# First image by half chunks, low rows loaded ahead into any stored place, and a reordered seam in a scan-then-pointwise kernel

## The chip, the cores and the metric

The kernel runs on one core of one Trainium2 chip. The metric is device time in microseconds (us). The core has a matmul engine (TensorE, PE in the profile, PEld for its weight loads), a vector engine (VectorE, DVE), an activation engine (ScalarE, ACT), a general engine (GpSimd, POOL) and a queue that only issues transfers (SyncE, SP). Each executes its own instruction list in order, and they meet at semaphores. Transfers between DRAM and on-chip memory are issued from SP, ACT or POOL and run on 16 shared DMA engines.

## What is computed

The input is 16 images of 128 channels by 64 x 64, float32. There are two residual layers, each on a group-normalised copy of its input (groups of 4 channels over a whole image):

```python
# layer 0: x = x + diagonal_lstm(_gn(x))    a scan over skewed columns, 64 rows in parallel
# layer 1: x = x + quantum_conv(_gn(x))     pointwise: each pixel on its own
xq = xf @ pre_w.T + pre_b                   # 128 channels -> 4 angles
z = _simulate(xq, q_weights)                # 4 qubits, 2 layers, expectation of Z
out = z @ post_w.T + post_b                 # 4 -> 128 channels
```

Layer 1's normalisation needs the mean and variance of each whole image after layer 0, so no pixel of layer 1 can start before layer 0's last pixel is known.

## The kernel before

**Storage.** Forty of the 64 rows of every image live on chip in `ring`, a tile of 10 blocks of 4 rows. The first 24 rows ("low rows") are finished early by the scan, are written out to a DRAM scratch `low`, and their blocks take the last 24 rows. In layer 1 an image is 8 chunks of 512 pixels (256 KB): chunks 0 to 2 (`k < NT`, with `NT` = 3) are low rows that must be loaded again, chunks 3 to 7 are pairs of blocks in `ring`.

**Layer 0** is 160 scan steps (`step`), bound by TensorE. After the last step, `residual(NSTEP - 1, ...)` adds the last diagonal to `x` in place (L618, on POOL), `late_sums` on POOL (L685 to L689) has gathered moments of the last rows, and the *seam* closes the statistics. A strip of the last 4 columns is summed on DVE (L894 to L898), TensorE adds the group sums (L883), DVE and ACT make `rstd2` (L902 to L904, then L149 to L153), DVE scales the angle weights of image 0 (`image_weights`, L913), and TensorE makes `mr_ps` (L925) for the bias `b_image` (L926). `fill()` (L183) is a matmul of 512 columns whose output nobody reads: one stands ahead of the strip's sum and two behind it.

**Layer 1**, per image `b`, all in an order written out by hand (`tc.manual_schedule()`: every engine gets its instructions in program order):

- `angles(b)`, PE L962: 8 matmuls of 32 output rows by 512 columns make the 128 angle rows `theta` from the 8 chunks. A float32 matmul shows as two records.
- `sines(b)`: ACT adds the bias (L976), DVE reduces to a turn (`near` L978, subtraction L979), ACT takes the sine (L982).
- `squares(b)`: 2 matmuls to amplitudes (`am`, L990) and 2 squares on ACT (L1002).
- `outputs(b, h)`, h = 0, 1: 4 matmuls `po` (L1008) into 4 PSUM banks, one per chunk.
- `finish(b, h, po)`: for each chunk, DVE adds output, bias and `x` in place (L1025), and SP stores it to `out_dram` (L1027).

The loop body for image `b` is `outputs(b,0)`, first half of `sines(b+2)`, `finish(b,0)`, loads, `squares(b+1)`, `outputs(b,1)`, `finish(b,1)`, `angles(b+3)`. The angles of an image are therefore made while three images are in flight.

**Low rows in layer 1.** The 48 low chunks go through 14 fixed places: 8 `spare` tiles and 6 `lowp` tiles. Chunks 0 to 13 are loaded in the seam, some from SP during the last steps, six from POOL. Later chunks always take the place of the chunk 14 before:

```python
lows[n] = spare[n % NBUF] if n % NBUF < 8 else lowp.tile(...)      # NBUF = 14
for n in range(NBUF + NT * b, min(NBUF + NT * b + NT, NT * NB)):   # in the loop, after finish(b, 0)
    load(n)                                                        # a DMA issued from POOL
```

Each such load waits on POOL until the store of the chunk that held the place has landed. The places of `ring` chunks are stored once and not used again.

Of the kernel before, what the change touches and what calls it, by code (L numbers as in the profile page):

```python
# [11 lines left out]
F32 = mybir.dt.float32  # L12
AF = mybir.ActivationFunctionType
# [3 lines left out]
P = 128  # L17
NB = 16
# [7 lines left out]
BLOCK = ROWS * NW  # L26
CHUNK = 2 * BLOCK
# [7 lines left out]
NSTEP = BAND + NW + SLOTS - 1  # L35
# [45 lines left out]
def kernel(  # L81
# [29 lines left out]
    NT = NLOW * NW // CHUNK  # L111
    low = dram.tile([NB, P, NLOW * NW], F32, name="low")
# [43 lines left out]
    with ExitStack() as scan:  # L156
# [5 lines left out]
        bias = wpool.tile([P, 4], F32, name="bias")  # L162
# [4 lines left out]
        xns, hst = ([v.rearrange("p (q n) -> p q n", q=2) for v in spare[i : i + 2]] for i in (4, 6))  # L167
# [8 lines left out]
            ps = pool.tile([P, v.shape[-1]], F32, name=nc.get_next_instruction_name(), tag=tag)  # L176
            nc.tensor.matmul(ps, lhsT=wsT[:, 0:P], rhs=v, start=True, stop=True)

        def fill():

            ps = ps_gate.tile([P, 512], F32, name=nc.get_next_instruction_name(), tag="gate")
            v = w_amp.rearrange("p h n -> p (h n)").unsqueeze(1).to_broadcast([P, 2, 256])
            nc.tensor.matmul(  # L183
                ps.rearrange("p (k n) -> p k n", k=2), lhsT=w_out, rhs=v, start=True, stop=True
            )

        def inv_step(j, pool):

# [27 lines left out]
        with ExitStack() as prep:  # L216
# [139 lines left out]
            for i in range(2):  # L356
                v = ws_n[i]
# [43 lines left out]
            first = {}  # L401
# [150 lines left out]
        def by_pairs(v, q, j, n):  # L552
            v = v[:, q, j * NB : (j + n) * NB]
            return v if n == 1 else v.rearrange("p (k h i) -> p k h i", h=2, i=NB)
# [53 lines left out]
            if a1 < b:  # L608
                nc.gpsimd.tensor_sub(diff[:, 0, a1:b], now[:, 1, a1 - NB : b - NB], now[:, 0, a1:b])  # L609

        def residual(t, new):

            for band in range(2):
                s0, s1 = slots(t, band)
                for q in range(2):
                    j0, j1 = (s0 + 1 - q) // 2, (s1 + 1 - q) // 2
                    for j, n, x1 in diagonal(t, band, q, j0, j1):
                        nc.gpsimd.tensor_add(x1, x1, by_pairs(new, q, j, n))  # L618
# [238 lines left out]

        def low_rows(queue, n, v):
            b, k = n // NT, n % NT
            queue.dma_start(out=v, in_=low[b, :, k * CHUNK : (k + 1) * CHUNK])  # L860

        waiting = []
        begin(nc.gpsimd.tensor_copy, cst, 0, cinv, 0)
# [1 line left out]
        with tc.manual_schedule():  # L865
# [6 lines left out]
            for later in sums:  # L872
                for _ in later:
                    pass
            residual(NSTEP - 1, hst[NSTEP % 2])
            low_rows(nc.sync, 6, spare[6])

            warm = small.tile([P, 1], F32, name="warm", tag="inv_t")
# [3 lines left out]
            def add(to, w, v, start=False):  # L882
                nc.tensor.matmul(to, lhsT=w, rhs=v, start=start, stop=True, skip_group_check=True)  # L883

            add(ps, by_half, moments, True)
            for h in range(2):
                add(ps, by_half, added[:, :, :, h])
                add(ps[:, 1], by_one, inner[:, :, h])
            fill()

            v = ring[:, block(NH - ROWS)].rearrange("p i (r w) -> p i r w", w=NW)[:, :, :, NW - STRIP :]
            d, sq = (work.tile([P, NB, ROWS, STRIP], F32, name=f"strip{i}", tag=f"both{i}") for i in range(2))
# [9 lines left out]
            nc.vector.tensor_copy(m, ps[:, 0])  # L902
            nc.vector.scalar_tensor_tensor(var, m, -1.0, m, ALU.mult, ALU.mult)
            nc.vector.scalar_tensor_tensor(var, var, EPS, ps[:, 1], ALU.add, ALU.add)  # L904
            for _ in range(2):
                fill()
            inverse_root(small, var, rstd2, 2)

            nc.scalar.activation(warm, shift, AF.Sin)
# [20 lines left out]

    lowp = ctx.enter_context(tc.tile_pool(name="lowp", bufs=6))
    sinp = ctx.enter_context(tc.tile_pool(name="sinp", bufs=3))
    nearp = ctx.enter_context(tc.tile_pool(name="nearp", bufs=1))
    sqp = ctx.enter_context(tc.tile_pool(name="sqp", bufs=2))
# [2 lines left out]
    ps_o = ctx.enter_context(tc.tile_pool(name="ps_o", bufs=1, space=PSUM))  # L939
    ths, turns, sqs = {}, {}, {}  # L940

    NBUF = 14
    lows = {}

    def load(n):

        lows[n] = spare[n % NBUF] if n % NBUF < 8 else lowp.tile([P, CHUNK], F32, name=f"low{n}", tag="low")
        if n >= 8:
            low_rows(nc.gpsimd, n, lows[n])

    def rows_of(b, k):
        if k < NT:
            return lows[NT * b + k]
        q = block(2 * ROWS * k)
        return ring[:, q : q + 2, b, :]

    def angles(b):
        th = ps_t.tile([P, CHUNK], F32, name=f"theta{b}", tag="theta")
        for h in range(2):

            for j in (2, 3, 1, 0):
                nc.tensor.matmul(  # L962
                    th[32 * j : 32 * j + 32, :],
                    lhsT=w_image[:, b, 16 - 16 * h : 48 - 16 * h],
                    rhs=rows_of(b, 2 * j + h),
                    start=(h == 0),
                    stop=(h == 1),
                    tile_position=(0, 32 * j),
                )
        ths[b] = th  # L970

    def sines(b):

        th = ths[b]
        y = sinp.tile([P, CHUNK], F32, name=f"y{b}", tag="y")
        nc.scalar.activation(y, th, AF.Identity, bias=b_image[:, b : b + 1])  # L976
        near = nearp.tile([P, CHUNK], F32, name=f"near{b}", tag="near")
        nc.vector.tensor_scalar(near, y, ROUND, ROUND, ALU.add, ALU.subtract)  # L978
        nc.vector.tensor_sub(y, y, near)  # L979
        turns[b] = y  # L980
        yield
        nc.scalar.activation(y, y, AF.Sin, scale=TWO_PI)  # L982

    def squares(b):
        ams = []
        for h in range(2):
            am = ps_a.tile([P, CHUNK], F32, name=f"am{b}_{h}", tag=f"am{h}")

            k = 64 * h
            nc.tensor.matmul(  # L990
                am,
                lhsT=w_amp[k : k + 64, h, :],
                rhs=turns[b][k : k + 64, :],
                start=True,
                stop=True,
                tile_position=(k, 0),
            )
            ams.append(am)

        sqs[b] = [sqp.tile([P, CHUNK], F32, name=f"sq{b}", tag="sq"), turns[b]]  # L1000
        for am, s in zip(ams, sqs[b]):
            nc.scalar.activation(s, am, AF.Square)  # L1002

    def outputs(b, h):
        po = [ps_o.tile([P, CHUNK], F32, name=f"po{b}_{h}_{j}", tag=f"po{j}") for j in range(4)]
        for j in range(4):
            k = 32 * j
            nc.tensor.matmul(  # L1008
                po[j],
                lhsT=w_out[k : k + 32, :],  # L1010
                rhs=sqs[b][h][k : k + 32, :],
                start=True,
                stop=True,
                tile_position=(k, 0),
            )
        return po

    def finish(b, h, po):
        for j in range(4):
            k = 4 * h + j  # L1020
            x1 = rows_of(b, k)
            y = po[j]
            if k >= NT:
                y = y.rearrange("p (k n) -> p k n", n=BLOCK)
            nc.vector.scalar_tensor_tensor(x1, y, b_out, x1, ALU.add, ALU.add)  # L1025
            o = ov[b, :, k * CHUNK : (k + 1) * CHUNK]
            nc.sync.dma_start(out=o if k < NT else o.rearrange("c (k n) -> c k n", n=BLOCK), in_=x1)  # L1027

    def idle():

# [73 lines left out]
```

## Time and profile before

| what | value |
|---|---|
| runs (3): median, lowest, highest | 1425.06, 1423.18, 1426.97 us |
| profiled execution: time, span of its instructions | 1422.99, 1421.1 us |
| mean granted TensorE clock | 0.997 |
| busy share of the span: PE, DVE, POOL, ACT | 96%, 69%, 65%, 55% |
| layer 1, first store issued to end of span | 1299.21 to 1421.1 us |
| in that stretch: mean rate of all transfers | 349 GB/s |

The runs differ among themselves by 0.27%; the profiled execution is 2.07 us under the median of the runs, and its span leaves out 1.89 us of its time. All positions below are us from the start of the span. "Share" of DMA is the mean busy share of the 16 DMA engines.

### The profile page before, as it was taken

Reading aid. Unit: us, or ns where it says so; the run is one execution under the profiler, and the core shown is the slowest. Engines: PE = TensorE matmul, PEld = TensorE weight load, DVE = VectorE, ACT = ScalarE, POOL = GpSimd, SP = SyncE. Lnnn points to the kernel's source line nnn. Section 1 sums busy time; section 2 is a strip of 40 time slices with the busy share of each in tenths; the row PEclk is TensorE's granted clock in tenths of the full one; section 3 lists DMA queues with packets and bytes.
Section 4 is the critical chain, followed back from the end, with each engine's and each line's share of the span. In section 5 each row is a group of like instructions: output and inputs, shape, how many; then the busy total and the mean of one; then the engine's idle time right before and its main releaser. Section 6 shows DMA issues by size and latency. Waiting matters only on the chain. (4 is left out here: it accounts for less than half of the span.)

```text
span 1421.1 us, 20142 instructions
## 1 busy us (share of the span) xinstructions
PE 1364.6 (96%) x5970; PEld 964.5 (68%) x5970; DVE 981.4 (69%) x2538; ACT 778.0 (55%) x1856; POOL 921.9 (65%) x1824
## 2 busy tenths in 40 slices
PE   6778999999999999999999999999999999888998
PEld 5658887777767777667666777776667778783332
DVE  7983555566665666887777776666665567866877
ACT  4555666555555555555555555555555566543331
POOL 4226887777667777788877776777777777762120
PEclk9999999999999999999999999999999999999999
DMA  9970000000000000133333100000000000005999
GB/s 332 368 272 1 1 2 0 1 1 1 1 0 1 0 1 1 59 119 119 119 119 119 60 1 1 0 1 1 1 1 0 2 1 1 31 9 200 369 373 324
DMA packets 88013, 107.05 MB, mean 75 GB/s; under 512 B 5424, under 2 KB 72016, under 8 KB 87904
## 3 DMA queue, kind: packets, MB, share of 16 engines
q1 hardware_dynamic: 83264, 94.39, 19.4%
q0 software_dynamic: 3408, 10.58, 2.2%
q8 instruction: 48, 0.79, 0.2%
q10 hardware_dynamic: 1232, 0.80, 0.2%
q14 instruction: 61, 0.50, 0.1%
HBM read 59.61 MB, written 46.14 MB: 74 GB/s over the span
## 5 line engine op out<-in xcount | busy, mean ns | idle before, releaser
L584 PE MATMUL ps<-spare,wxT 128*128 128x512 f32 (+18 forms) x1280 | 479.6, 518 | 0.7 <-POOL spare L575 0.7
L768 DVE TENSOR_TENSOR ps<-ps,both 128x256 f32<-128x256 f32 (+9 forms) x544 | 221.8, 409 | 304.7 <-PE ps L753 303.1
L772 ACT ACTIVATE ps<-ps,bias 128x512 f32<-128x512 f32 (+23 forms) x480 | 279.3, 583 | 220.2 <-DVE ps L768 183.7
L753 PE MATMUL ps<-spare,w1T 128*128 128x256 f32 (+16 forms) x1272 | 345.8, 353 | 9.9 <-DVE spare L835 4.9
L584 PEld LDWEIGHTS ps<-spare,wxT 128*128 128x128 f32 x1280 | 230.9, 190 | 173.2 <-issue 155.5
L753 PE MATMUL ps<-spare,w0T 128*128 128x256 f32 (+16 forms) x1272 | 343.8, 352 | 0.8 <-POOL spare L609 0.8
L803 ACT COPY both<-ps 128x256 f32<-128x256 f32 (+9 forms) x544 | 191.6, 355 | 180.7 <-PE ps L753 161.1
L618 POOL TENSOR_TENSOR ring<-ring,spare 128x256 f32<-128x256 f32 (+8 forms) x488 | 248.1, 540 | 31.2 <-DVE stats L706 21.0
L753 PEld LDWEIGHTS ps<-spare,w1T 128*128 128x128 f32 x1272 | 229.8, 190 | 35.7 <-DVE spare L835 7.6
L753 PEld LDWEIGHTS ps<-spare,wsT 128*128 128x128 f32 x1088 | 194.8, 190 | 86.4 <-DVE spare L835 34.7
L753 PE MATMUL ps<-spare,wsT 128*128 128x256 f32 (+14 forms) x1088 | 241.3, 365 | 5.4 <-DVE spare L835 3.7
L753 PEld LDWEIGHTS ps<-spare,w0T 128*128 128x128 f32 x1272 | 230.3, 190 | 22.1 <-POOL spare L609 0.9
L575 POOL TENSOR_TENSOR spare<-spare,rstd 128x512 f32<-128x512 f32 (+10 forms) x160 | 171.0, 1069 | 14.8 <-DVE rstd L153 2.3
L570 POOL TENSOR_TENSOR spare<-ring 128x256 f32<-128x256 f32 (+8 forms) x213 | 147.5, 703 | 0.0
L829 ACT ACTIVATE g<-cst 128x256 f32<-128x256 f32 (+20 forms) x320 | 103.1, 369 | 64.4 <-DVE cst L828 63.8
L835 DVE TENSOR_TENSOR spare<-g,ps 128x256 f32<-128x256 f32 (+17 forms) x319 | 105.6, 369 | 43.8 <-ACT g L829 41.9
L565 POOL TENSOR_TENSOR spare<-ring,mean 128x16 f32<-128x16 f32 (+8 forms) x247 | 131.3, 541 | 5.8 <-DVE mean L143 5.6
L609 POOL TENSOR_TENSOR spare<-spare 128x240 f32<-128x240 f32 (+9 forms) x136 | 102.7, 755 | 29.5 <-DVE spare L835 25.7
L772 ACT ACTIVATE g<-ps,bias 128x512 f32<-128x512 f32 (+20 forms) x160 | 97.4, 609 | 27.1 <-DVE ps L768 21.1
L828 DVE TENSOR_TENSOR cst<-cst,ps 128x256 f32<-128x256 f32 (+20 forms) x320 | 104.6, 368 | 5.5
L855 POOL COPY spare<-spare 128x16 f32<-128x16 f32 x64 | 21.1, 330 | 134.0 <-DVE spare L835 134.0
L825 DVE TENSOR_TENSOR ps<-ps,g 128x512 f32<-128x512 f32 (+20 forms) x160 | 95.1, 595 | 17.0 <-ACT g L772 16.6
(341 smaller groups left out, 1120.4 us busy)
## 6 DMA issues: line engine op xcount, KB each, us to landing
ring<-in_x_dram SPq DMA_DIRECT2D x80, 256.0 KB, 5.6
out_dram<-ring SPq DMA_DIRECT2D x80, 256.0 KB, 5.1
low<-ring SPq DMA_DIRECT2D x6, 2048.0 KB, 7.5
ring<-in_x_dram SPq DMA_DIRECT2D x6, 2048.0 KB, 8.1
out_dram<-spare SPq DMA_DIRECT2D x30, 256.0 KB, 5.2
spare<-in_x_dram SPq DMA_DIRECT2D x27, 256.0 KB, 5.5
spare<-low POOLq DMA_DIRECT2D x22, 256.0 KB, 5.3
rest<-in_x_dram SPq DMA_DIRECT2D x21, 256.0 KB, 5.6
```

What stands on the lines that cost most here:

```text
L565: nc.gpsimd.tensor_sub(by_pairs(xn, 0, j, n), x0, over(mean1, n))
L570: nc.gpsimd.tensor_sub(by_pairs(xn, 1, j, n), lower, of)
L575: nc.gpsimd.tensor_mul(v, v, r)
L584: nc.tensor.matmul(ps[g][:, :, a:b], lhsT=wxT[:, g * 128 : (g + 1) * 128], rhs=xns[t % 2][:, :, a:b], start=t > 0, stop=True, skip_group_c ...
L618: nc.gpsimd.tensor_add(x1, x1, by_pairs(new, q, j, n))
L753: nc.tensor.matmul(out, lhsT=w[:, g * 128 : (g + 1) * 128], rhs=rhs, start=False, stop=True, skip_group_check=True,)
L768: nc.vector.tensor_add(v, v, both[g][:, a:b])
L772: nc.scalar.activation(to[:, :, a:w], ps[g][:, :, a:w], FUNC[g], bias=bias[:, g : g + 1])
L803: nc.scalar.copy(both[g][:, a:b], ps[g][:, 0, a:b])
L828: nc.vector.tensor_add(c[:, q], c[:, q], ig[:, q])
L829: nc.scalar.activation(th[:, q, a:w], c[:, q], AF.Tanh)
L835: nc.vector.tensor_mul(new[:, q, a:v], th[:, q, a:v], act[GO][:, q, a:v])
```

## The change

Four things are altered.

1. **Seam.** The last `residual` runs on DVE instead of POOL. `fill(n)` issues `n` matmuls of 256 columns; there are two ahead of the late sums' matmuls, one behind these, and four (where there were two of 512 columns) behind the strip's sum.
2. **First image by halves.** `angles`, `sines`, `squares`, `outputs` and `finish` take an optional half `c`: the same work on 256 of a chunk's 512 columns. Image 0 runs as two such halves, written out ahead of the loop, with the angles of images 1, 2 and 3 placed between; the loop starts at image 1. Its stores are 16 of 128 KB instead of 8 of 256 KB.
3. **Places.** `places` is a first-in-first-out list of every chunk stored, the five `ring` chunks of an image too. `load(n)` takes the next `n` places for the next `n` low chunks, whatever image they are of.
4. **Pace of loads.** `load(3)` after `finish(b, 0)` and `load(2)` after `finish(b, 1)`, five per image instead of three, until all 48 chunks have a place.

```diff
-        def fill():
+        def fill(n):
...
+            for _ in range(n):
+                ps = ps_gate.tile([P, 256], F32, name=nc.get_next_instruction_name(), tag="gate")
+                v = w_amp.rearrange("p h n -> p (h n)")
+                nc.tensor.matmul(ps, lhsT=w_out, rhs=v, start=True, stop=True)
...
-        def residual(t, new):
+        def residual(t, new, engine=nc.gpsimd):
...
-                        nc.gpsimd.tensor_add(x1, x1, by_pairs(new, q, j, n))
+                        engine.tensor_add(x1, x1, by_pairs(new, q, j, n))
...
-            residual(NSTEP - 1, hst[NSTEP % 2])
+            residual(NSTEP - 1, hst[NSTEP % 2], nc.vector)
             low_rows(nc.sync, 6, spare[6])
...
             add(ps, by_half, moments, True)
+            fill(2)
             for h in range(2):
                 add(ps, by_half, added[:, :, :, h])
                 add(ps[:, 1], by_one, inner[:, :, h])
-            fill()
+            fill(1)
...
-            for _ in range(2):
-                fill()
+            fill(4)
             inverse_root(small, var, rstd2, 2)
...
-    lowp = ctx.enter_context(tc.tile_pool(name="lowp", bufs=6))
+    lowp = ctx.enter_context(tc.tile_pool(name="lowp", bufs=1))
...
-    NBUF = 14
-    lows = {}
+    places = list(spare) + [lowp.tile([P, CHUNK], F32, name=f"low{i}") for i in range(6)]
+    lows = []
 
     def load(n):
 
-        lows[n] = spare[n % NBUF] if n % NBUF < 8 else lowp.tile([P, CHUNK], F32, name=f"low{n}", tag="low")
-        if n >= 8:
-            low_rows(nc.gpsimd, n, lows[n])
+        while n and places and len(lows) < NT * NB:
+            v = places.pop(0)
+            lows.append(v)
+            if len(lows) > 8:
+                low_rows(nc.gpsimd, len(lows) - 1, v)
+            n -= 1
...
+    def half(v, c):
+
+        if c is None:
+            return v
+        return v[:, c] if len(v.shape) == 3 else v[:, c * BLOCK : (c + 1) * BLOCK]
+
-    def angles(b):
-        th = ps_t.tile([P, CHUNK], F32, name=f"theta{b}", tag="theta")
+    def angles(b, c=None):
+        th = half(ps_t.tile([P, CHUNK], F32, name=f"theta{b}_{c}", tag="theta"), c)
...
-                    rhs=rows_of(b, 2 * j + h),
+                    rhs=half(rows_of(b, 2 * j + h), c),
...
-    def finish(b, h, po):
+    def finish(b, h, po, c=None):
         for j in range(4):
             k = 4 * h + j
...
+            v = rows_of(b, k)
+            x1, y, o = half(v, c), po[j], ov[b, :, k * CHUNK : (k + 1) * CHUNK]
+            if c is not None:
+                o = o[:, c * BLOCK : (c + 1) * BLOCK]
...
             nc.vector.scalar_tensor_tensor(x1, y, b_out, x1, ALU.add, ALU.add)
...
+            nc.sync.dma_start(out=o, in_=x1)
+            if c != 0:
+                places.append(v)
...
     with tc.manual_schedule():
-        for n in range(NBUF):
-            load(n)
-        angles(0)
-        for _ in sines(0):
-            pass
+        load(len(places))
+
+        first = []
+        for c in range(2):
+            angles(0, c)
+            first.append(sines(0, c))
+        for _ in range(2):
+            for later in first:
+                next(later, None)
+        squares(0, 0)
+        po = outputs(0, 0, 0)
+        finish(0, 0, po, 0)
+        squares(0, 1)
+        po = outputs(0, 1, 0)
         angles(1)
+        finish(0, 1, po, 0)
         later = sines(1)
         next(later)
-        squares(0)
+        po = outputs(0, 0, 1)
         next(later, None)
-        for b in range(NB):
+        finish(0, 0, po, 1)
+        load(3)
+        squares(1)
+        po = outputs(0, 1, 1)
+        finish(0, 1, po, 1)
+        load(2)
+        angles(2)
+        for _ in sines(2):
+            pass
+        angles(3)
+        for b in range(1, NB):
             po = outputs(b, 0)
-            later = sines(b + 2) if 0 < b < NB - 2 else iter(())
+            later = sines(b + 2) if b + 2 < NB else iter(())
             finish(b, 0, po)
-            for n in range(NBUF + NT * b, min(NBUF + NT * b + NT, NT * NB)):
-                load(n)
+            load(3)
...
             finish(b, 1, po)
-            if b == 0:
-                angles(2)
-                for _ in sines(2):
-                    pass
+            load(2)
             if b + 3 < NB:
                 angles(b + 3)
```

More of the change, by code (lines that the diff above doesn't have):

```diff
@@ L177, in keep @@
             nc.tensor.matmul(ps, lhsT=wsT[:, 0:P], rhs=v, start=True, stop=True)
-        def fill():
[L181 to L185, printed above, removed]
+        def fill(n):
[3 more added lines that the diff above has]
+                nc.tensor.matmul(ps, lhsT=w_out, rhs=v, start=True, stop=True)
         def inv_step(j, pool):
@@ L859, in low_rows @@
             b, k = n // NT, n % NT
-            queue.dma_start(out=v, in_=low[b, :, k * CHUNK : (k + 1) * CHUNK])
+            of = low[b, :, k * CHUNK : (k + 1) * CHUNK]
+            queue.dma_start(out=v, in_=of if len(v.shape) == 2 else of.rearrange("p (k n) -> p k n", n=BLOCK))
         waiting = []
@@ L969, in angles, with sines, squares @@
                 )
[L970 to L977, printed above, removed]
+        ths[b, c] = th
+    def sines(b, c=None):
+        if b not in turns:
+            turns[b] = sinp.tile([P, CHUNK], F32, name=f"y{b}", tag="y")
+        y = half(turns[b], c)
+        nc.scalar.activation(y, ths[b, c], AF.Identity, bias=b_image[:, b : b + 1])
+        near = half(nearp.tile([P, CHUNK], F32, name=f"near{b}_{c}", tag="near"), c)
         nc.vector.tensor_scalar(near, y, ROUND, ROUND, ALU.add, ALU.subtract)
         nc.vector.tensor_sub(y, y, near)
-        turns[b] = y
         yield
         nc.scalar.activation(y, y, AF.Sin, scale=TWO_PI)
-    def squares(b):
+    def squares(b, c=None):
         ams = []
+        y = half(turns[b], c)
         for h in range(2):
-            am = ps_a.tile([P, CHUNK], F32, name=f"am{b}_{h}", tag=f"am{h}")
+            am = half(ps_a.tile([P, CHUNK], F32, name=f"am{b}_{h}_{c}", tag=f"am{h}"), c)
             k = 64 * h
@@ L992, in squares @@
                 lhsT=w_amp[k : k + 64, h, :],
-                rhs=turns[b][k : k + 64, :],
+                rhs=y[k : k + 64, :],
                 start=True,
@@ L998, in squares, with outputs @@
             ams.append(am)
[L1000 to L1005, printed above, removed]
+        if b not in sqs:
+            sqs[b] = [sqp.tile([P, CHUNK], F32, name=f"sq{b}", tag="sq"), turns[b]]
+        for am, v in zip(ams, sqs[b]):
+            nc.scalar.activation(half(v, c), am, AF.Square)
+    def outputs(b, h, c=None):
+        po = [
+            half(ps_o.tile([P, CHUNK], F32, name=f"po{b}_{h}_{j}_{c}", tag=f"po{j}"), c)
+            for j in range(4)
+        ]
         for j in range(4):
@@ L1010, in outputs @@
                 lhsT=w_out[k : k + 32, :],
-                rhs=sqs[b][h][k : k + 32, :],
+                rhs=half(sqs[b][h], c)[k : k + 32, :],
                 start=True,
@@ L1016, in outputs @@
         return po
-    def finish(b, h, po):
+    def finish(b, h, po, c=None):
         for j in range(4):
             k = 4 * h + j
[L1021 to L1024, printed above, removed]
+            v = rows_of(b, k)
+            x1, y, o = half(v, c), po[j], ov[b, :, k * CHUNK : (k + 1) * CHUNK]
+            if c is not None:
+                o = o[:, c * BLOCK : (c + 1) * BLOCK]
+            elif len(v.shape) == 3:
+                y, o = (u.rearrange("p (k n) -> p k n", n=BLOCK) for u in (y, o))
             nc.vector.scalar_tensor_tensor(x1, y, b_out, x1, ALU.add, ALU.add)
-            o = ov[b, :, k * CHUNK : (k + 1) * CHUNK]
-            nc.sync.dma_start(out=o if k < NT else o.rearrange("c (k n) -> c k n", n=BLOCK), in_=x1)
+            nc.sync.dma_start(out=o, in_=x1)
+            if c != 0:
+                places.append(v)
     def idle():
```

## Prediction

> **What bounds the kernel now.** I read the page's slices first, then the chain of waits from 1225 us on, then the timeline of layer 1, then busy time in short stretches of the seam and of layer 1.
>
> The slices (section 2 of the page, one digit per 35.5 us) place layer 1: DMA is full only in the read-in at the front and in the last four slices. The change touches only this end.
>
> ```profile
> PE   6778999999999999999999999999999999888998
> ...
> DMA  9970000000000000133333100000000000005999
> ```
>
> The chain of waits names the seam. Columns: start, duration, what.
>
> ```profile
> 1284.36 0.25 POOL ring L618
> 1284.62 0.02 issue
> 1284.64 0.43 DVE strip L894
> ...
> 1286.23 0.62 PE gm L883 x2
> 1286.86 1.87 PE I-10725_10726 L183 x2
> 1288.72 1.40 PE I-10728_10729 L183 x2
> 1290.13 0.10 issue
> 1290.23 1.18 PE theta L962 x8
> ```
>
> The strip waits for POOL's last residual. Then two fillers last until 1290.13, though the weights of image 0 (L913) are ready at 1288.86. They are slow because the clock is halved; next to last columns are clock, DMA share, GB/s:
>
> ```profile
> 1285.50:1286.00 0.50, 0.00 (x0) 0.00 (x0) 0.50 (x3) 0.00 (x0) 0.50 (x2) 1.00 0.94 328
> ...
> 1286.50:1287.00 0.50, 0.50 (x3) 0.50 (x4) 0.11 (x1) 0.00 (x0) 0.50 (x2) 0.50 1.07 377
> ```
>
> In layer 1 the timeline shows TensorE's weight loads for `theta` waiting for low rows, and POOL, which must load them, waiting for the store that frees the place:
>
> ```profile
> 1333.70 0.11 PEld L962 LDWEIGHTS theta<-low,w_image 128*32 128x32 f32 x1 [1.63 <-DMA low<-low]
> ...
> 1356.62 0.11 PEld L962 LDWEIGHTS theta<-spare,w_image 128*32 128x32 f32 x2 [1.55 <-DMA spare<-low]
> ...
> 1374.03 0.54 POOL L860 DMA_DIRECT2D low<-low  x1 [5.69 <-DMA out_dram<-low]
> ...
> 1380.28 0.11 PEld L962 LDWEIGHTS theta<-low,w_image 128*32 128x32 f32 x2 [2.39 <-DMA low<-low]
> ```
>
> Is DMA then the bound? Stretches of layer 1 say: only in the middle. It carries nothing between the seam's loads and the first store (1299.21), is full from 1330 to 1400 (375 GB/s), and goes slack in the tail, where loads are over and compute sets the pace.
>
> ```profile
> 1290.00:1300.00 10.00, 8.20 (x54) 2.59 (x53) 3.97 (x8) 3.99 (x7) 0.00 (x0) 1.00 0.06 23
> ...
> 1350.00:1360.00 10.00, 9.36 (x47) 3.05 (x48) 6.86 (x12) 3.09 (x5) 2.92 (x5) 1.00 1.06 385
> ...
> 1400.00:1410.00 10.00, 10.00 (x34) 3.56 (x31) 9.37 (x15) 1.91 (x4) 0.00 (x0) 1.00 0.89 313
> ```
>
> **The sum's base.** All steps are against the profiled span of 1421.1 us. That execution took 1422.99, 2.07 under the median of 1425.06; I apply the difference found to the median. "Within 0.3%" (4.3 us) is about what a measurement of this kernel can tell from no change.
>
> **Seam (about -2.7 us at the first theta).** The last diagonal is one 128x16 addition. On POOL it runs at 1284.36, behind the late sums and one low load of 0.65. On DVE it follows the L835 that ends at 1282.91; DVE rows of that size take 0.17 to 0.18, so the strip starts near 1283.2, its 1.54 (1284.64 to 1286.18) end near 1284.75, against 1286.18. Only the strip is queued behind the addition on DVE. SP's load of chunk 6 also waited for the POOL residual and goes earlier; POOL's six loads lose one neighbour. Both gain at most 0.2 and hide, since images 2 and 3 need them later.
>
> Fillers: three of 512 columns (1536) become seven of 256 (1792). At full clock 512 took 1.10, so 0.55 each. Two fit the hole of 1.17 on PE (1282.05 to 1283.22) ahead of the late sums, one covers 1284.15 to 1284.7, four run from the strip's sum (1285.2 with its matmul at 0.4) to 1287.4. The vector chain from `m` (1286.89) to the weights (1288.86) takes 1.97, so weights are ready at 1287.2. Theta then starts at 1287.5, not 1290.23. This rests on the clock staying up: the stretch of 3.4 us before the drop was 60% busy in the rows above and becomes over 90%.
>
> **First image by halves (-6.1 us for the first store, but +1.5 us for image 1).** Half durations from rows: ACT 128x256 0.37 (L829), DVE `near` 0.29 and subtraction 0.38 (halves of 0.43 and 0.69 with their fixed part kept), theta 16 records in 1.1, `am` and `po` 0.55 each, one L1025 0.41 against 0.66 to 0.69. From 1287.5: theta half and `mr_ps` to 1289.0; y0 to 1289.5, turn to 1290.2; ACT's order is y0, y1, sine 0, sine 1, squares, so sine 0 ends at 1290.9, sine 1 at 1291.7, the first square at 1292.05; `po` to 1292.65, first store at 1293.1 against 1299.21. SP needs 0.34 to issue one (1351.87), under the 0.41 at which DVE makes halves, so 16 issues hide.
>
> The rest does not shift as far. `angles(1)` waits for `po(0,1)` (end 1294.6) and ends at 1296.6; its y, turn and sine end at 1299.2, behind them `finish(0,0)` second half (to 1300.1), `am(1)`, `po(0,1)`, then `angles(2)` and `angles(3)`, 1.9 each, to 1304.65 and `po(1,0)` 1.1. `finish(1,0)` starts at 1305.8; before, at 1307.0. So 2.7 in the seam minus 1.5 leaves 1.2.
>
> **A rule against this.** PE is idle for 2.1 us (1297.15 to 1299.25) in this order. The Trainium skill, "TensorE: Matmul & The Clock Gate", Part 1, says that the clock halves after an idle window of about 3.4 us, and its table warns of gaps over 3 us; by that, nothing happens here. The trace disagrees: the clock halved for 3.41 us (1286.28 to 1289.69) after a stretch that was 60% busy with no gap above 1.2, while 70% busy stretches (21.25 to 24.65; 1293.0 to 1296.4) kept it. A 3.41 us window that holds the new gap is under 45% busy, and windows of four phases in five hold enough of it. I take the trace: half clock over `angles(2)` and part of `angles(3)`, +1.5. `finish(1,0)` is back at 1307.3. By the rule the sum would be 1.5 lower.
>
> **Low rows ahead (about -8 us).** Between `finish(1,0)` and `finish(15,0)` before: 1411.47 - 1307.0 = 104.47. Intervals with hardly a wait: 6.84, 6.85, 6.97, 6.91, 6.90, mean 6.89; fourteen make 96.5. The difference, 8.0, agrees with the PEld waits for loads: 0.43, 1.63, 0.45, 1.55, 0.29, 2.39, 0.16, 0.26, sum 7.2. With 8 places freed per image and 34 loads left, POOL runs ahead: chunk 14 takes image 0's first place (stored by 1302, landing about 1307) and is needed by `angles(4)` at 1309.6, the tightest; later ones have several images in hand. POOL's waits stay long, but only loads are queued behind them.
>
> The sum: 1307.3 + 96.5 + the old tail of 9.63 (1411.47 to 1421.1) = 1413.4.
>
> **The DMA floor.** 33.55 MB of stores and 34 loads of 0.262 make 42.5 MB after the first store (before: 121.9 us x 349 GB/s, the same). From 1293.8 at 375 GB/s 113.3 us, 3 us lost while image 0 is slow, 2.1 from last byte (1419.0) to the end: 1412.2, just under compute. Loads go first, stores queue some 10 us deep around image 5, and the tail, where compute makes 2.1 MB per 6.9 us, drains it. "DMA: Bandwidth & Descriptors", Specifications, gives about 358 GB/s of DRAM per core; by that the floor is 1417.7. The trace held 375 over 70 us, so 375 stands, and the other goes into the range. Unknown: loads into `ring` in pieces of 1 KB. Before has none in this direction from `low`; nearest are read-in into ring blocks, 350 to 400 GB/s in 70 to 95 us, so I take zero, between -1 and +4.
>
> **Rivals.**
>
> *DMA takes over* (25%): the removed waits come back as stores queued at the end. With the mean rate of before from first store to last byte, 42.5 MB / 119.85 us = 354 GB/s, idle parts in it, the end is 1293.8 + 120 + 2.1 = 1416; with the page's 358 and the 3 us, 1417.7. Time 1420 to 1422. For it: share 1.0 in most of layer 1. Against: tail at 313.
>
> *Clock stays up and DMA keeps pace* (18%): 1411.9 or a little less, time about 1415 and down to 1411.5.
>
> *Lookahead idle* (4%): waits belong to other causes and only the start counts; -1.2 to -2.7, time 1423. Against: the named waits.
>
> *Slower* (3%): loads, front-loaded and split, mix so badly with stores that the rate falls. At a mean of 340 GB/s, as in 1302 to 1320 (share 1.00), 125 us make the end 1420.9, no change; from 328 down (129.6 us, end 1425.5) it is slower by over 0.3%; at 325 the time is 1430.7. Against: the 340 came with dips of demand, and 1350 to 1360 with five loads ran at 385.
>
> **The numbers.** Likeliest (50%): -7.7, 1417.4, own range 1415.5 to 1420. Range 1411.5 to 1421.8. Faster by over 0.3% (below 1420.8): 0.50 + 0.18 + 0.18 of the DMA case = 0.86; slower 0.03; same 0.11.
>
> **What would show it.** First theta at 1287.5 and no 0.50 clock before it; first store 1293; a clock drop around 1299 to 1303; no `theta` wait on DMA after image 3; all low loads issued by about 1350; DMA share near 1 to the last 10 us; intervals of `finish(b,0)` at 6.9. Wrong if: intervals exceed 7.2 without waits on loads, the last store lands over 3 us behind the last DVE addition, or `angles(4)` waits for chunk 14.

## The result and the profile after

| | median, lowest, highest (us) | runs | ratio to before, 95% |
|---|---|---|---|
| before | 1425.06, 1422.56, 1426.97 | 7 | |
| after | 1420.86, 1419.52, 1423.24 | 7 | 0.9971 [0.9959, 0.9983] |

The change saves 4.1 us by the ratio (its interval is 2.4 to 5.8 us). Forecast was 7.7. The profiled execution of after took 1420.86, the median itself, with a span of 1419.1. Of the runs below, the kernel with few `ring` places has six executions, of which one took 1777.96 at a clock of 0.752; its ratio is made without it (the median of the other five is 1417.13).

One thing about positions first. Layer 0, which the change does not touch, ended at 1282.91 (end of the last L835) in the profile of before and at 1284.94 (the same line, now L834) in that of after; in the eleven profiles of whole kernels used here it lies anywhere between 1282.91 and 1286.17. Part of the 2.03 is a half clock of 3.41 us at 102.86, in layer 0 of after; the profile of before has the clock at 1.00 there. So spans of single profiles cannot be subtracted. I count from that end: "+10" is 10 us after layer 0's last DVE row. Layer 1 then took 138.19 before and 134.16 after, 4.03 less, which agrees with the ratio. `finish(b,h)` in the table stands for the start of its first addition.

| from the end of layer 0 | before | after | predicted |
|---|---|---|---|
| first theta | +7.32 | +4.56 | +4.6 |
| first store issued | +16.30 | +10.42 | +10.2 |
| finish(1,0) | +24.1 | +23.3 | +24.4 |
| finish(15,0) | +128.6 | +119.3 | +120.9 |
| last DVE addition ends | +133.9 | +124.9 | +126.2 |
| from there to the end of the span | 4.3 | 9.3 | 4.3 |
| end | +138.2 | +134.2 | +130.5 |

All rows of compute came out within 0.2 us of the forecast or earlier. The last addition is 9.0 us earlier than before, and then 5.0 of them are given back: the last stores are not through. Counted for the transfers alone: from the first store to the last landing, the same 42.6 MB took 120.6 us before (353 GB/s) and 122.5 after (348). They began 5.9 earlier and ran 1.9 longer, and the difference is what was saved.

The slices of after: the last DMA digits are full as before, but the last PE digit has fallen from 8 to 6. TensorE is done and transfers go on.

```profile
PE   6778999999999999999999999999999999888996
...
DMA  9980000000000000133333100000000000005999
```

The chain of waits through the seam (start, duration, what). The residual, now on DVE, starts at once behind L834; the strip follows; the chain runs to the weights on DVE and ACT without a filler in it.

```profile
1284.77 0.18 DVE spare L834
...
1284.98 0.28 DVE ring L617
...
1285.35 0.44 DVE strip L895
...
1286.94 0.42 PE gm L883 x2
...
1289.18 0.17 DVE w_image L913
...
1289.50 0.64 PE theta L972 x8
```

The chain's end: its last piece is a DVE addition that ends at 1409.84, 9.26 us ahead of the end of the span.

```profile
1403.11 1.11 PE po_None L1023 x8
1404.21 0.74 DVE ring L1042
...
1405.10 3.97 PE po_None L1023 x8
...
1409.09 0.75 DVE ring L1042
```

What is behind it, SP's timeline shows. Here a row is a run of issues: start, length, how many. SP has hardly a gap from 1398.68 on, and it is still issuing at 1415.2, over 5 us after DVE's last result. Fifteen stores take 11.31, one every 0.75. The issue itself takes 0.65 (median of the last twelve from `ring`), where the first eight of image 0 in the trace before took 0.33 to 0.57. That reads as a store waiting at issue for room; the runs with two queues below test it.

```profile
1398.68 11.31 SPq L1043 DMA_DIRECT2D out_dram<-ring  x15
1410.09 1.39 SPq L1043 DMA_DIRECT2D out_dram<-low  x2
1411.56 3.66 SPq L1043 DMA_DIRECT2D out_dram<-ring  x5
```

Busy time in stretches (the stretch and its length; busy us of PE, PEld, DVE, ACT and POOL with the number of instructions; clock, DMA share, GB/s):

```profile
1295.40:1310.00 14.60, 12.53 (x93) 4.62 (x92) 9.89 (x22) 5.63 (x11) 3.05 (x5) 1.00 0.66 211
1310.00:1370.00 60.00, 60.00 (x318) 20.37 (x317) 56.06 (x89) 20.96 (x35) 18.92 (x29) 1.00 1.05 386
1370.00:1417.00 47.00, 38.13 (x166) 13.02 (x164) 36.31 (x56) 10.01 (x17) 0.00 (x0) 0.89 1.02 347
```

Three stretches, three rates. DMA starts slowly (share 0.66), then runs above the forecast's 375 while low rows are loaded between the stores (the last of them lands at 1354), and falls to 347 at a full share when only stores are left. From 1310 to 1400 TensorE has no gap (10.00 of every 10 us), so it does not wait for the transfers, and the transfers end later.

### The profile page after: what moved, and what is told of

It reads as the page before. It is cut to its first block, busy times and chain, and to the rows that moved or that the text cites. A ratio compares the mean times of both kernels' runs of the same rounds, so it can differ in the third digit from the quotient of the medians.

```text
span 1419.1 us, 20261 instructions
## 1 busy us (share of the span) xinstructions
PE 1358.3 (96%) x6014; PEld 964.4 (68%) x6014; DVE 982.4 (69%) x2549; ACT 778.4 (55%) x1860; POOL 924.6 (65%) x1823
## 5 line engine op out<-in xcount | busy, mean ns | idle before, releaser
L834 DVE TENSOR_TENSOR spare<-g,ps 128x256 f32<-128x256 f32 (+17 forms) x319 | 105.5, 368 | 43.7 <-ACT g L828 41.8
L854 POOL COPY spare<-spare 128x16 f32<-128x16 f32 x64 | 21.1, 329 | 134.2 <-DVE spare L834 134.2
```

What stands on the lines that cost most here:

```text
L834: nc.vector.tensor_mul(new[:, q, a:v], th[:, q, a:v], act[GO][:, q, a:v])
```

## The experiments

Each kernel was timed beside before, on the same chip. Four are built from parts of the change and were timed together, so that their times can be set against each other too.

**The seam alone.** Before, with part 1 of the change only.

```diff
-            residual(NSTEP - 1, hst[NSTEP % 2])
+            residual(NSTEP - 1, hst[NSTEP % 2], nc.vector)
...
+            fill(2)
...
-            fill()
+            fill(1)
...
-            for _ in range(2):
-                fill()
+            fill(4)
```

> The kernel before with the seam's part of the change alone (last residual on VectorE, seven fillers of 256 columns); image 0 whole and the 14 fixed places as before. All theories: first theta 2.7 us earlier counted from the last L835 addition. Theory A (transfers are the bound from the first store on, so an earlier first store is kept): end 2.5 to 3 us earlier than before. Theory B (compute with its waits for low rows is the bound in the middle): the same shift, but 0 to 2 us are given back as waits, since loads do not come earlier by as much; end 1 to 2.5 earlier.

Measured: 1424.72 against 1426.53, ratio 0.9990 [0.9982, 0.9999], so 1.4 us, with an interval that goes down to 0.1. Theta starts at +4.56, as in after: the 2.76 are there. But the last DVE addition stays at +134.0 (before +133.9), and layer 1 takes 138.0 (before 138.2), so the profile shows hardly any of the 1.4. The waits of `theta` for low rows grow to 10.0 us (before 7.1), as the lists of waits of the weight loads show (us in total, times, longest; first two rows before, then this run):

```profile
PEld theta L962 <- DMA low<-low: 4.0, 2, 2.4
PEld theta L962 <- DMA spare<-low: 3.1, 6, 1.6
...
PEld theta L961 <- DMA spare<-low: 5.2, 5, 2.4
PEld theta L961 <- DMA low<-low: 4.8, 3, 2.2
```

An earlier start alone mostly waits longer for the same loads.

**The residual alone.** Before with the one line `residual(NSTEP - 1, hst[NSTEP % 2], nc.vector)`; the three old fillers stay.

> The kernel before with the last residual on VectorE alone; the three long fillers stay. If the fillers' length and place are what kept the clock up: it falls to 0.50 in the seam as before, the strip's sum is 1.4 us earlier from layer 0's end, but the first theta only 1.0 to 1.5 earlier (5.8 to 6.3 after layer 0's end, against 4.56 with the new fillers). If the earlier strip alone closed the gap on TensorE: no fall of the clock and the first theta at 4.6 to 5.0.

Measured: theta at +6.08, that is 1.24 of the 2.76. It ran once (1424.39, before 1426.72), so only its positions count. The clock still falls, in the same place:

```profile
1286.00:1288.00 2.00, 2.00 (x5) 1.10 (x4) 0.48 (x3) 0.00 (x0) 2.00 (x5) 0.50 0.97 309
1288.00:1290.00 2.00, 2.00 (x4) 0.53 (x2) 1.51 (x10) 1.66 (x3) 0.32 (x1) 0.73 0.98 277
```

In after the row 1285.00:1289.50 has the clock at 1.00. So of the seam's gain the place of the addition is 1.24, the fillers and with them the clock 1.5.

**No halves: image 0 as before, all else of the change.**

```diff
-        first = []
-        for c in range(2):
...
-        for b in range(1, NB):
+        angles(0)
+        for _ in sines(0):
+            pass
         angles(1)
         later = sines(1)
         next(later)
+        squares(0)
+        next(later, None)
+        for b in range(NB):
...
+            if b == 0:
+                angles(2)
+                for _ in sines(2):
+                    pass
```

> The changed kernel with image 0 whole again, in the order of before; seam and places of the change are kept. Theory A: the halves made the first store 3 us earlier but left the transfer engines half empty until image 1 (183 and 206 GB/s in the 20 us after the first theta); with a whole image 0 more bytes have moved 20 us after the first theta, and the end is 1 to 3 us earlier than the changed kernel, so 5 to 7 under before. Rival H (the halves pay: what counts is the first store): 2 to 3 us later than the changed kernel, so 1 to 2 under before.

Measured: 1418.78 (1416.71 to 1420.46), ratio 0.9948 [0.9933, 0.9963], 7.4 us saved, where the whole change saved 4.1. The first store is 3.1 us later than in after (+13.55), and still by +32 the transfers have moved 8.27 MB, against 7.49. The last addition is 2.3 earlier than in after (+122.6), and from the first store to the last landing the transfers take 117.8 us (after 122.5). The halves begin sooner and then starve: their second stores wait for `angles(1)` and its sines, and a place is free only when both halves are stored. POOL's timeline of after has its first load for a freed place at 1303.73, 18.8 us into the layer; with image 0 whole it is at +16.1:

```profile
1303.73 1.61 POOL L860 DMA_DIRECT2D spare<-low  x3 [14.72 <-DMA out_dram<-spare]
```

**No lookahead: parts 1 and 2 of the change, with only low chunks' places and three loads per image, as before.**

```diff
-            if c != 0:
+            if c != 0 and k < NT:
                 places.append(v)
...
-        load(2)
         angles(2)
...
-            load(2)
             if b + 3 < NB:
```

> The changed kernel with the 14 places of before (only stored low chunks are reused, three loads per image); seam and halves are kept. Theory A: the waits of theta for low rows come back (6 to 8 us in sum), but stores were queued anyway; the end moves by less than 1.5 us against the changed kernel. Rival C (the prediction's: lookahead takes 8 us of waits off the path): the end is 5 us or more later than the changed kernel, that is 1 or more later than before.

Measured: 1427.54, ratio 1.0007 [0.9998, 1.0015]. `theta` waits 12.4 us for low rows, the last DVE addition is at +138.2, and the tail behind it is 3.9 (before 4.3).

```profile
PEld theta_None L972 <- DMA spare<-low: 9.3, 4, 3.3
...
PEld theta_None L972 <- DMA low<-low: 3.1, 3, 2.0
```

The theory that transfers alone set the end, so that these waits are worth nothing, is wrong here: without the lookahead the waits come back, and the kernel is slower by 6.8 us than the next one, which has it. The forecast's step was right.

**The loads spread out.** After with three loads per image (five for image 0), each group held on POOL until DVE has written the last stored chunk (a copy of one column), so that loads are issued until 1375 instead of 1348.

```diff
+        if done and len(lows) < NT * NB:
+            nc.gpsimd.tensor_copy(tick, done[-1])
...
-            load(3)
+            load(2)
...
-            load(2)
+            load(1)
```

> The changed kernel with loads spread: five for image 0, then three per image, each batch held back on GpSimd by a copy of one column of the chunk just finished; places as changed. Loads then last to about image 10 instead of image 5. Rival M (stores alone run at 345 GB/s and beside loads at 400, so bunching the loads wastes the tail): 3 us earlier than the changed kernel, 7 under before. Theory A in its plain form (the bytes cost the same in any order, since loads beside stores are nearly free wherever they stand): within 1 us of the changed kernel.

Measured: 1420.76, ratio 0.9962 [0.9949, 0.9976]; after's median is 1420.86. The end of compute (+125.1) and the tail (8.9) are those of after. From the first store to the last landing it moves 348 GB/s, as after does. When the loads run makes no difference that can be seen; the 3 us of the rival are not there.

These four make a table. The kernel with the loads spread out stands for after in it:

| | without lookahead | with lookahead | lookahead is worth |
|---|---|---|---|
| image 0 whole | 1424.72 | 1418.78 | 5.9 |
| image 0 by halves | 1427.54 | 1420.76 | 6.8 |
| the halves cost | 2.8 | 2.0 | |

Lookahead brings about 6 us, and the halves take back 2 to 3. The smallest step, 2.0, is the difference of two sets of runs that hardly overlap (1416.71 to 1420.46, and 1419.83 to 1423.42). The lengths of layer 1 in the four profiles (138.0, 132.6, 142.1, 134.0) have the same signs: lookahead 5.4 and 8.1, halves 4.1 and 1.4.

**The halves finished in a row.** To see whether the interleaving is at fault: both halves of image 0 are finished ahead of `angles(1)`; its sines, `angles(2)` and `squares(1)` come behind that.

```diff
-        angles(1)
         finish(0, 1, po, 0)
-        later = sines(1)
-        next(later)
         po = outputs(0, 0, 1)
-        next(later, None)
         finish(0, 0, po, 1)
...
         load(2)
+        angles(1)
+        later = sines(1)
+        next(later)
         angles(2)
+        next(later, None)
+        squares(1)
```

> The changed kernel with the two halves of image 0 finished one after the other: the angles and sines of images 1 to 3 come behind the last half store, not between. Theory A (what counts is how many bytes have moved early, not when the first store goes): all of image 0 is stored 6 us after its first store, which stays 10.4 after layer 0's end; 32 us after layer 0's end 8.5 to 9 MB have moved, against 7.5 in the changed kernel and 8.3 with a whole image 0; the end is 1 to 2 us earlier than with a whole image 0, about 9 under before. Rival H2 (halves cost compute at the start and the end follows the compute): image 1 starts late and the end is no earlier than the changed kernel.

Measured: 1420.94, ratio 0.9955 [0.9938, 0.9971]: no better than after by its median (1420.86). Image 0 is indeed out sooner (SP has issued its last store at 1301.8, +18.2, where in after the second halves run to 1306.0, +21.0), but then nothing is ready to be stored until 1310.74, and by +32 only 7.42 MB have moved. On top of that the clock falls:

```profile
1295.60:1299.60 4.00, 4.00 (x22) 2.63 (x24) 3.88 (x10) 0.00 (x0) 0.00 (x0) 0.84 0.79 266
1299.60:1303.60 4.00, 4.00 (x20) 0.90 (x24) 0.48 (x1) 0.33 (x1) 3.04 (x5) 0.50 0.76 211
...
1307.60:1311.60 4.00, 3.15 (x24) 0.74 (x16) 2.85 (x5) 2.29 (x5) 1.12 (x2) 1.00 0.58 168
```

My theory of more bytes by +32 was wrong. The hole only moves: in both orders tried, image 1 is late while image 0 is by halves. Part of this run's loss is the clock: its last addition is at +127.7 (after +124.9), and order and clock are not separated here.

**Transfers by themselves.** A kernel of transfers only: stages of 96 to 160 stores of 256 KB from one place, some with loads between; it computes nothing, and ran once.

```python
for n in range(96):
    store(n, whole)      # 2 KB pieces per partition, as a `spare` place; `halves`: two pieces of 1 KB, as two blocks of `ring`
```

> None of the computation: only transfers, in six stages with a barrier between. (1) 96 stores of 256 KB in pieces of 2 KB, (2) 96 in pieces of 1 KB, (3) as 1 with a load of 256 KB in pieces of 2 KB after each sixth store, (4) as 2 with such loads in pieces of 1 KB, (5) 64 stores in pieces of 1 KB with 32 loads of 2 KB, (6) 128 stores of 2 KB. Rival P (piece size sets the rate of stores): stage 2 at about 345 GB/s, stage 1 at 385 or more. Rival M (the direction sets it): stages 1 and 2 both near 345, stages 3 to 5 at 370 to 400.

The loads of the later stages ran ahead, most of them into the first. Its stretch 20 to 40 has stores of 2 KB pieces with loads, the last of them issued at 30.5; in 40 to 60 only the stores are left. 120 to 140 has stores alone in pieces of 1 KB, 200 to 220 in pieces of 2 KB; 280 to 300 has stores alone in pieces of 1 KB, just behind another run of loads (columns: stretch, length, DVE, POOL, clock, DMA share, GB/s):

```profile
20.00:40.00 20.00, 0.00 (x0) 8.19 (x12) 1.00 1.04 408
40.00:60.00 20.00, 0.00 (x0) 0.00 (x0) 1.00 1.05 406
...
120.00:140.00 20.00, 0.00 (x0) 0.00 (x0) 1.00 1.02 342
...
200.00:220.00 20.00, 0.00 (x0) 0.00 (x0) 1.00 1.01 382
...
280.00:300.00 20.00, 0.00 (x0) 0.00 (x0) 1.00 1.08 374
```

This is the missing number. A share of 1.0 is not one rate: 342 GB/s for stores from `ring`-like places, 382 from `spare`-like ones, and about 400 with loads among them. But the loads among them are not the whole of it. The first and the third stage write the same 96 chunks of DRAM from the same place on chip; behind the loads the first still runs at 406 (405 up to 70 us), the third, with no loads ahead of it, at 382. Stores of 1 KB pieces run at 374 behind loads and at 342 in the next 20 us. So a raised rate outlasts the loads by some 20 us or more, and the cause of that is not known. After's tail (347) is mostly the first kind (87% of its store bytes go in pieces of 1 KB); its middle (386) is the mix and what follows it. The page's list of issues shows that the change makes the slow kind more frequent, 95 whole chunks from `ring` and 10 halves, against 80 whole chunks before, because low rows now lie in `ring` places too:

```profile
out_dram<-ring SPq DMA_DIRECT2D x95, 256.0 KB, 3.7
...
ring<-low POOLq DMA_DIRECT2D x20, 256.0 KB, 6.8
```

Twenty chunks more (5.24 MB) at 342 instead of 382 are 1.6 us by these rates (15.3 - 13.7), an estimate.

**Two queues.** The same stages with 1 KB and 2 KB pieces on SP alone, on SP and ACT, and on SP and POOL, stores only; it computes nothing, and ran once.

> None of the computation: only stores of 256 KB, 96 in each of six stages with a barrier between and 128 at the end: from SyncE alone, from SyncE and ScalarE in turn, from SyncE and GpSimd in turn, each first in pieces of 1 KB, then of 2 KB; the last stage SyncE alone, 2 KB. Rival Q (one issuing queue cannot keep the transfer engines full; loads lifted the rate because they came from a second queue): two queues give 380 GB/s or more in 1 KB pieces, 400 in 2 KB pieces, against 342 and 382. Rival M (the mix of reads and writes lifts the rate): two queues change nothing, 342 and 382 in all stages.

SP and ACT give what SP gives; SP and POOL less. Rows: SP with 1 KB; SP and ACT with 1 KB; SP and POOL with 1 KB, then 2 KB (columns as above).

```profile
20.00:40.00 20.00, 0.00 (x0) 0.00 (x0) 1.00 1.03 341
...
180.00:200.00 20.00, 0.00 (x0) 0.00 (x0) 1.00 1.04 340
...
340.00:360.00 20.00, 0.00 (x0) 6.63 (x10) 1.00 0.96 316
...
420.00:440.00 20.00, 0.00 (x0) 5.50 (x11) 1.00 1.02 368
```

So a single issuing queue is not what holds stores at these rates, and SP's long issues in the tail are the sign of full engines, not their cause.

**Few `ring` places.** Image 0 whole, and of the `ring` chunks only the first six stored give their places to low rows.

```diff
-            if c != 0:
+            if c != 0 and (k < NT or len(taken) < 6):
                 places.append(v)
+                if k >= NT:
+                    taken.append(v)
```

> The changed kernel with image 0 whole, and only the first six stored ring chunks lent as places (20 places in rotation instead of a growing list); seam as changed. Loads then keep to three per image, and most low chunks are stored in pieces of 2 KB. Rival P: 1.5 to 2 us earlier than with a whole image 0 and all places. Rival M: 2 to 3 us earlier, since loads last to the end. Theory A in its plain form: the same within 1 us.

Measured: 1417.18, ratio 0.9928 [0.9908, 0.9947]: 10.3 us under before, the best median of all, and under both kernels. No `theta` waits for a load; the tail is 9.4 (the kernel with image 0 whole: 10.0). The rate near the end is a little better, 355 over 20 us (first row), where image 0 whole has 342 and 349 (the two other rows; 347 over 1396 to 1416):

```profile
1393.00:1413.00 20.00, 11.30 (x39) 3.84 (x34) 10.91 (x16) 1.08 (x2) 0.00 (x0) 0.75 1.03 355
...
1400.00:1408.00 8.00, 6.41 (x21) 2.16 (x20) 6.66 (x11) 0.00 (x0) 0.00 (x0) 0.93 1.02 342
1409.00:1416.00 7.00, 0.00 (x0) 0.00 (x0) 0.00 (x0) 0.00 (x0) 0.00 (x0) 0.50 1.02 349
```

That it beats the kernel with image 0 whole (1418.78) is likely but not shown: the intervals of the two ratios overlap, and layer 1 is hardly shorter in its profile (132.3 against 132.6). Eight chunks fewer from `ring` (92 against 100) would be worth 0.6 by the rates above.

**Stores on POOL as well.** Image 0 whole, and from image 7 on every second store is issued by POOL. Then the same on the kernel with few `ring` places, from image 11 on.

```diff
-            nc.sync.dma_start(out=o, in_=x1)
+            (nc.gpsimd if b > 6 and k % 2 else nc.sync).dma_start(out=o, in_=x1)
```

> The changed kernel with image 0 whole, and from image 7 on, when the low loads are over, every second chunk is stored from GpSimd instead of SyncE. Rival Q: the last 50 us run at 380 GB/s instead of 345, the end is 4 to 5 us earlier than with a whole image 0 (12 under before), and the last store lands about 5 us behind the last addition instead of 10. Rival M: no change within 1 us.

> As the kernel with six ring places and a whole image 0, but from image 11 on every second chunk is stored from GpSimd. Rival Q: the stores-only tail of some 30 us runs at 385 instead of 353 GB/s, 2 to 3 us earlier than without, about 12 under before. Rival M: no change within 1 us.

Measured: 1420.83, ratio 0.9959 [0.9944, 0.9974], and 1420.45, ratio 0.9957 [0.9941, 0.9972]: 2.0 and 3.3 us above the medians of the kernels they were made from. The intervals of the ratios overlap in both pairs, so a loss is likely and not shown; the gain of 4 to 5 us that rival Q foresaw did not come. In the first the last DVE addition is where it was (+122.6), and the tail is 11.6 instead of 10.0, at this rate:

```profile
1376.00:1416.00 40.00, 29.93 (x129) 10.50 (x128) 29.43 (x46) 7.61 (x13) 14.07 (x21) 0.90 1.01 335
```

## Why the prediction was right, and where it was not

The measured time lies inside the full range, but outside the 1415.5 to 1420 of the case called likeliest; it is where a rival stood.

**Seam: right.** -2.76 against -2.7, by the mechanism given. What it missed is that the seam alone is worth about half of that (1.4, interval 0.1 to 2.6), because `theta` gives the rest back to the loads.

**First store: right in time (-5.9 against -6.1), wrong in worth.** The prediction gave image 1 a delay of 1.5 and got 2.0 (first theta to `finish(1,0)`, 16.77 before and 18.75 after). It did not ask what they do to the transfers, beyond "3 us lost while image 0 is slow". From 1295.4 to 1310 they moved 211 GB/s; at 375 that is 6.4 us lost (14.6 x 164 / 375). With image 0 whole 0.8 MB more are through by +32, and the time is 2.0 lower than with halves (the table above).

**Half clock: wrong.** TensorE does sit idle as foreseen, but the rows of after have the clock at 1.00 through that hole; this one has PE busy for 1.93 of 4.00 us, with a gap of 2.07. The kernels without lookahead and with the loads spread out have the same hole (1.94 of 4.00) and the same clock, so it was not one lucky execution:

```profile
1299.00:1303.00 4.00, 1.93 (x20) 0.74 (x19) 2.69 (x6) 1.34 (x3) 0.00 (x0) 1.00 0.35 118
```

Here the rule of the Trainium skill, "TensorE: Matmul & The Clock Gate", Part 1 (an idle window of about 3.4 us) predicted the right thing and my reading of a busy share did not; +1.5 fell away. In the seam of before, and with the halves in a row, the rule as written does not hold: the clock fell with no gap above 1.2 us. In layer 0 of after it fell at 102.86, behind 3.41 us that were 55% busy with a gap of 1.37, and it kept up over the 3.41 us from 1299.00, 39% busy. In the first two the stretch ahead was thinly filled: in the seam, few matmuls and small ones; in the other, matmuls of 256 columns paced by DVE, eight records of `po` in 1.78 to 2.30 us that take 0.71 where nothing holds them. In after, full `theta` matmuls of 1.95 us stand between. That it is the work in the array that counts, and not the recorded share or a gap, fits these two and the hole, but was not tested.

**Lookahead: right.** `finish(1,0)` to `finish(15,0)` took 95.95 against a forecast of 96.5, no `theta` waited on a load, and the loads were issued by 1348. `angles(4)` did not wait for chunk 14. Worth 5.9 to 6.8 of the forecast's 8: what is missing is what transfers take.

**The old tail of 9.63 and the DMA floor: the step that failed.** "42.5 MB ... at 375 GB/s ... 1412.2, just under compute", "375 stands", and "the tail, where compute makes 2.1 MB per 6.9 us, drains it". By the mark that the prediction set ("the last store lands over 3 us behind the last DVE addition") it was wrong: the last store lands 8.0 behind it, and the 9.63 from `finish(15,0)` to the end measured 14.9. Against the floor, with the rates that were measured: the slow start cost 6.4 instead of 3; the middle at 386 gave back 1.8 (60 x 11 / 375); the tail at 347 cost 3.5 (47 x 28 / 375). Together 5.1 over the forecast's floor, which puts the floor at +134.4 from the end of layer 0 (1412.2 is +129.3); the measured end is +134.2. (The sum closes because the measured rates go into it; it shows where the time went, not why.) The 375 was a mean over a stretch of before in which every image had three loads among its stores. Stores alone, well behind the last load, are slower (342 and 382 by themselves, 347 in the tail). That the lookahead takes the loads out of the end is not what costs the time, though: spread out to 1375 they gave the same end. Drained at 347, with compute making 2.1 MB per 6.9 us (304), the queue shrinks by only 43 GB/s: 40 us take off 1.7 MB, and at 1409.84, when compute was done, there were still 2.6 MB, about 7.4 us of transfers, to come.

The prediction did have the number: its row of 313 GB/s in the tail of before had share 0.89, and 313 / 0.89 is 352. It read the row as slack and did not divide.

The rival "DMA takes over" had the mechanism (the removed waits come back as stores queued at the end) and the time (1420 to 1422, measured 1420.86), at 25%. The 358 of the Trainium skill ("DMA: Bandwidth & Descriptors", Specifications) gave 1417.7, +134.8, and came close to the end, but no kind of transfer measured by itself ran at it: those gave 342, 382 and about 400, and it is near because it lies between. That nearness is luck. Compute came out 1.3 earlier than forecast (mostly no half clock), and the tail behind it 5.0 longer; the difference, 3.7, is what the forecast was too low by. The 1.3 bought no time, since the stores end last.

Of the smaller readings, the slices show DMA full in the last three, not four, and the floor at 358 comes to 1417.6.

**What stays open.** After the last load the rate does not fall at once, as in the kernel of transfers alone. With the loads spread out, the last is issued at 1375 and lands at 1380.6, but 1385 to 1395 still moves 379 GB/s, almost all of it in pieces of 1 KB, and only 1395 to 1405 is down to 355:

```profile
1385.00:1395.00 10.00, 10.00 (x49) 3.51 (x49) 9.51 (x16) 3.58 (x7) 0.00 (x0) 1.00 1.08 379
1395.00:1405.00 10.00, 9.88 (x36) 3.43 (x36) 8.01 (x13) 1.63 (x3) 0.00 (x0) 1.00 1.04 355
```

Neither piece sizes nor queues explain that. Nor is it known why the loads cost the same in total at either place.

## What to carry to other kernels

Before taking waits off a compute chain, work out what the transfers behind it can do in each stage by itself: divide GB/s by share, and keep stages with loads, stores and both apart, since a full share stood for anything from 342 to 408 GB/s here. When compute gets ahead of transfers, an early first store is worth only the bytes that follow it: count what has moved by a fixed time, not when the first store leaves. And a place that comes free early is not free of cost if stores from its layout are slower (342 against 382 here).

## What was unexpected of the hardware

- Stores of 256 KB from on-chip memory run at 341 to 342 GB/s in pieces of 1 KB and 381 to 382 in pieces of 2 KB per partition, and mixed with loads at about 400 to 408, all at a share of 1.01 to 1.06.
- The higher rate stays for a while when the loads are over: 2 KB stores alone at 405 to 406 for 30 us, 1 KB stores alone at 374 for 20 us, then 342.
- A second queue adds nothing when the share is full (SP and ACT 339 to 340 and 380 to 382), and POOL as second issuer lowers the rate (304 to 325 and 365 to 368, at a share of 0.95 to 1.02).
- When the engines are full, SP's issue of a store stretches from 0.33 to 0.38 us to about 0.65. It looks like a slow issuer and is a full one.
- TensorE's clock stayed up over a hole of 2.07 us with half of 4 us empty, and fell behind the busier stretches named above, which had no gap above 1.4 us.
